# Second-layer steps of a two-layer graph attention kernel placed among the first layer's lists, with stored partial sums and a closing on ScalarE

## The chip, the cores and the metric

The kernel runs on one core of one Trainium2 chip. A core has five engines, each with an in-order queue of its own: TensorE (PE, matmuls; weight loads are listed as PEld), VectorE (DVE), ScalarE (ACT), GpSimd (POOL) and SyncE (SP), which here only issues transfers (DMA). The metric is device time in microseconds (us), the median of several runs.

## What is computed

There are 4096 nodes with 256 features and a sparse symmetric adjacency matrix (about one entry in 128 set, the diagonal always). Two graph attention layers follow each other, each with a residual and a layer norm:

```python
# layer 0: 8 heads of 128
Wh = einsum('nf,hfd->hnd', x, W_heads)
e  = leaky(s1[:, :, None] + s2[:, None, :], 0.2)     # s1, s2: Wh against a1, a2
att = softmax(where(adj > 0, e, NEG), axis=-1)
feat = elu(einsum('hnm,hmd->hnd', att, Wh))          # heads side by side
x = layernorm(x + feat @ W_out + b_out)
# layer 1: 4 heads of 64, the same adjacency
xt = einsum('ni,hio->hno', x, W)
e  = leaky(src[:, :, None] + dst[:, None, :], 0.2)
h  = einsum('hij,hjf->hif', softmax(where(adj > 0, e, -inf)), xt)
x = layernorm(x + heads side by side of h)
```

## The kernel before

In both layers the exponential of a leaky sum is taken as the larger of two products, so that a weight is two or three elementwise operations and no exponential for each pair. A row of ones beside the values gives the softmax's sums.

**First layer, sparse.** The 4096 targets are cut into 32 tiles of 128, each tile into 8 groups of 16 targets; a group is a *list* n = 0 to 255. For each list the nodes that are neighbours of any of its 16 targets are known as indices, and POOL gathers their table rows (256 features, factors, adjacency words: 305 floats) by indirect transfers: four of 128 rows for each list (`gather`, L777), and one more for four lists together (`Shared`, L791). DVE weighs them (`weigh`, L905 to L915), PE multiplies weights and rows into one PSUM bank (`gathered`, L918; L923), DVE inverts the sum and ACT divides (`invert`, `divide` L945, L947), PE transposes and ACT copies (`flip`, L950 to L957). The tile's own 128 rows come as `Near` (L835). When a tile's 8 lists are done, `close0` (L962) projects its heads (L981), applies elu, projects again (L1004), adds and normalises, and writes the tile's rows to DRAM (`x1_d`, L1028) and their transpose to `x1T` (L1032).

**Lists of neighbours.** For each of eight phases of 32 lists, `words_of` loads 16 blocks of adjacency (512 KB each, L508), turns them into 0 or 1 on ACT (two passes, L515 and L516) and packs the bits of 16 targets into words by matmuls (L528). `lists_of` picks the set nodes out of them on DVE (L594, L595) and publishes words and factors in the table.

**Order.** The first layer's order is written out by hand: one loop over n (L1097) emits, for each list, its pieces and those of neighbouring lists at fixed distances, a piece of counting, a piece of picking and one or two pieces of the queue `late`, which holds the closings and the second layer's scores and projections (`prepare1`, L744, L759, L768). Each engine gets its instructions in the order of this emission.

**Second layer, dense.** It begins when the loop has ended. For two pairs of heads g, four quarters of targets c (1024 each) and 32 source tiles j there is a *step*: load 512 KB of transposed adjacency on SP (L1181), turn it into an upper limit on ACT (L1182), weigh on DVE for both heads (L1310), and multiply on PE into three PSUM banks that accumulate over the 32 j: eight matmuls for values (L1200), four for sums (L1212), each of 32 columns, side by side in the array, each as two instructions. That is 256 steps. After each (g, c) the banks are copied, transposed back, divided and added to `y_sb` by DVE (`unit1`, L1222, L1250); with the second g each tile is normalised on DVE with a power on POOL (`layernorm`, L430 to L438) and stored. Here a scheduler orders the instructions.

The step's multiplications are these:

```python
for q in range(NQ):
    for b in range(2 * D1 // DQ):
        k, d = divmod(b * DQ, D1)
        nc.tensor.matmul(po[q][ts(b, DQ), :], wh[:, j, k, d : d + DQ],
                         es[k][:, ts(q, HB)], start=(j == 0), stop=(j == NT - 1), ...)
```

PSUM has eight banks: two each of `o0` (lists), `o1` (closings, scores) and `o2` (counting) in the pool `ps_o`, which the second layer uses for its sums, and two of `m` in `ps_m`.

Of the kernel before, what the change touches and what calls it, by code (L numbers as in the profile page):

```python
# [18 lines left out]
P = 128  # L19
# [243 lines left out]
def fast_path(  # L263
# [18 lines left out]
    CT = CH // P  # L282
# [21 lines left out]
    big = ctx.enter_context(tc.tile_pool(name="big", bufs=1))  # L304
    wpool = ctx.enter_context(tc.tile_pool(name="wh", bufs=1))
    apool = ctx.enter_context(tc.tile_pool(name="adj", bufs=4))
    small = ctx.enter_context(tc.tile_pool(name="small", bufs=4))
    ps_o = ctx.enter_context(tc.tile_pool(name="ps_o", bufs=2, space=PSUM))
    ps_m = ctx.enter_context(tc.tile_pool(name="ps_m", bufs=2, space=PSUM))
    first = ctx.enter_context(ExitStack())  # L310
    keep0 = first.enter_context(tc.tile_pool(name="keep0", bufs=1))
# [16 lines left out]
    xT_sb = big.tile([P, KC, N], F32, tag="xT", name="xT_sb")  # L328
    bad = const.tile([P, 6], F32, name="bad")
    nc.gpsimd.memset(bad, 0.0)  # L330
    rd_all = const.tile([P, NT * GT], F32, name="rd_all")

# [3 lines left out]
    class Scores:  # L336
# [38 lines left out]
        def chunk(self, k, src):  # L375
# [4 lines left out]
            def scores():  # L380
                ps = held["ps"] = ps_o.tile([P, CT, 2, H], F32, tag="o1", name=f"ps_{n}_{k}")
                for t in range(CT):
                    for c in range(KC):
                        nc.tensor.matmul(  # L384
                            ps[:, t],
                            src[:, c, ts(k * CT + t, P)],
                            self.v[:, c],
                            start=(c == 0),
                            stop=(c == KC - 1),
                        )  # L390
# [21 lines left out]
            def rows():  # L412
# [4 lines left out]
                nc.scalar.dma_start(self.r_d[k].rearrange("h t p -> (h t) p"), row)  # L417
# [11 lines left out]

    def layernorm(n, i, y):  # L430
        st = small.tile([P, nc.vector.BN_STATS_DIM], F32, tag="st", name=f"st_{n}_{i}")
        nc.vector.bn_stats(st, y)
        mv = small.tile([P, nc.vector.BN_AGGR_DIM], F32, tag="mv", name=f"mv_{n}_{i}")
        nc.vector.bn_aggr(mv, st)
        rstd = small.tile([P, 1], F32, tag="rstd", name=f"rstd_{n}_{i}")
        nc.vector.tensor_scalar(rstd, mv[:, 1:2], EPS, None, ALU.add)  # L436
        nc.gpsimd.tensor_tensor(rstd, rstd, neg_half, ALU.pow)  # L437
        nc.vector.tensor_scalar(y, y, mv[:, 0:1], rstd, ALU.subtract, ALU.mult)  # L438

# [58 lines left out]
    def words_of(s):  # L498

        pw = words[s] = []  # L500
        raw, bins = {}, {}
        NW = PT * NQ0

        def load(m):
            i, q = s * PT + m // NQ0, m % NQ0
            raw[m] = apool.tile([P, QN], I32, tag="aq", name=f"aq_{i}_{q}")
            queue = nc.scalar if s == 0 and m % 2 else nc.sync
            queue.dma_start(raw[m], adj[ts(i, P), ts(q, QN)])  # L508

        def convert(m):  # L510
            mb = two.tile([P, QN], BF16, tag="mb", name=f"mb_{s}_{m}", bufs=3)
            if s == 0:
                nc.vector.tensor_scalar(mb, raw.pop(m), 0.0, None, ALU.is_gt)
            else:
                nc.scalar.activation(mb, raw.pop(m), AF.Relu)  # L515
                nc.scalar.activation(mb, mb, AF.Sign)  # L516
            bins[m] = mb

        def count(m):

            t, q = divmod(m, NQ0)
            if m == 0:
                pw.extend(
                    ps_o.tile([P, 512], F32, tag="o2", name=f"pw_{s}_{k}") for k in range(QN // 512)
                )
            mb = bins.pop(m)
            for k in range(QN // 512):
                nc.tensor.matmul(  # L528
                    pw[k][ts(q, GP), :],
                    word[:, t, :],  # L530
                    mb[:, ts(k, 512)],
                    start=(t == 0),
                    stop=(t == PT - 1),
                    tile_position=(0, q * GP),
                    skip_group_check=True,
                )
# [861 lines left out]
```

## Time and profile before

| | us |
|---|---|
| median of three runs | 2705.93 (2693.68 to 2710.3) |
| span of the profiled execution | 2577.5 |
| first gather / last gather issued | 98 / 1779 |
| last list's matmuls begin | about 1803 |
| first / last matmul of the second layer | 1833 / 2555 |
| granted TensorE clock, mean | 0.924 |

The span runs from the first to the last instruction of one profiled execution; the timed runs are some 128 us longer. Busy time over the span: PE 2186.5 us (85%), DVE 1854.4 (72%), POOL 1201.6 (47%), ACT 1029.5 (40%). A matmul's listed duration contains its latency and overlaps the next one's, so PE's pace is read from counts in a stretch rather than from durations. In the rows below "idle before" is the time that the engine stood idle ahead of such an instruction, with what ended it.

### The profile page before, as it was taken

Reading aid. Unit: us, or ns where it says so; the run is one execution under the profiler, and the core shown is the slowest. Engines: PE = TensorE matmul, PEld = TensorE weight load, DVE = VectorE, ACT = ScalarE, POOL = GpSimd, SP = SyncE. Lnnn points to the kernel's source line nnn. Section 1 sums busy time; section 2 is a strip of 40 time slices with the busy share of each in tenths; the row PEclk is TensorE's granted clock in tenths of the full one; section 3 lists DMA queues with packets and bytes.
Section 4 is the critical chain, followed back from the end, with each engine's and each line's share of the span. In section 5 each row is a group of like instructions: output and inputs, shape, how many; then the busy total and the mean of one; then the engine's idle time right before and its main releaser. Section 6 shows DMA issues by size and latency. Waiting matters only on the chain.

```text
span 2577.5 us, 37206 instructions
## 1 busy us (share of the span) xinstructions
PE 2186.5 (85%) x12585; PEld 1281.6 (50%) x12585; DVE 1854.4 (72%) x3802; ACT 1029.5 (40%) x2577; POOL 1201.6 (47%) x1156
## 2 busy tenths in 40 slices
PE   6368888888878888888788887878999999999997
PEld 4235565555555555556555565655543432324433
DVE  4547668667656667755776766555699799999997
ACT  0075535435533543553453233332444544334332
POOL 1356677677566677657767767774000000010110
PEclk9978889999888898888998989998999999999998
DMA  9597556557455646655765644442766566666653
GB/s 279 148 299 181 164 156 188 161 158 192 136 151 135 203 132 154 193 143 139 199 182 147 134 115 137 120 129 75 241 223 195 165 203 211 210 200 220 190 179 98
DMA packets 212958, 443.64 MB, mean 172 GB/s; under 512 B 60819, under 2 KB 125462, under 8 KB 212758
## 3 DMA queue, kind: packets, MB, share of 16 engines
q1 hardware_dynamic: 152982, 261.55, 34.4%
q0 software_dynamic: 52224, 169.97, 23.2%
q10 hardware_dynamic: 7552, 9.65, 1.1%
q8 instruction: 102, 1.67, 0.3%
q14 instruction: 98, 0.80, 0.1%
HBM read 426.04 MB, written 23.40 MB: 174 GB/s over the span
## 4 chain that ended last, share of the span: by engine, by line
PE 61%; DMA 14%; DVE 10%; ACT 6%; POOL 4%; issue 4%; ACTq 0%; DVEq 0%; POOLq 0%; SPq 0%
PE po L923 24%; PE po L1200 17%; DMA G<-table,ids 12%; PE po L1212 8%; POOL G L783 3%; PE ph L981 3%; PE py L1004 3%; ACT ag L947 2%; PE pw L528 2%; PE ps L384 2%; DVE e L908 1%; DVE e L914 1%; DVE e L915 1%; PE pw L759 1%; ACT el L991 1%
## 5 line engine op out<-in xcount | busy, mean ns | idle before, releaser
L783 POOL DMA_INDIRECT G<-table,ids x1024 | 1083.4, 1058 | 586.3 <-issue 354.3
L1310 DVE SCALAR_TENSOR_TENSOR e<-rb,pj,mb 128x1024 f32<-128x1024 f32 x512 | 631.2, 1279 | 44.3 <-PE po L1212 24.4
L923 PE MATMUL po<-G,e 128*128 128x257 f32 x2048 | 620.5, 455 | 13.1 <-DVE e L915 12.9
L1200 PE MATMUL po<-e,wh 128*32 128x512 f32 x4096 | 623.5, 594 | 6.5 <-DVE e L1310 6.0
L923 PEld LDWEIGHTS po<-G,e 128*128 128x128 f32 x2048 | 433.3, 222 | 179.3 <-issue 38.3
L1212 PE MATMUL po<-e,cj 128*32 128x512 f32 x2048 | 464.2, 592 | 0.0
L1182 ACT ACTIVATE mb<-aq 128x1024 bf16<-128x1024 int32 x256 | 270.7, 1058 | 412.9 <-DVE e L1310 353.3
L923 PE MATMUL po<-own,eo 128*128 128x257 f32 x512 | 184.5, 444 | 285.9 <-ACT ag L947 271.0
L437 POOL TENSOR_TENSOR rstd<-rstd,neg_half 128x1 f32<-128x1 f32 x32 | 28.4, 891 | 722.9 <-DVE rstd L436 533.7
L1200 PEld LDWEIGHTS po<-e,wh 128*32 128x32 f32 x4096 | 199.9, 110 | 281.7 <-issue 196.3
L923 PEld LDWEIGHTS po<-own,eo 128*128 128x128 f32 x512 | 82.3, 202 | 324.9 <-ACT ag L947 310.4
L915 DVE TENSOR_TENSOR e<-e,mbs 128x512 f32<-128x512 f32 x256 | 177.4, 693 | 65.9 <-ACT mbs L902 43.4
L923 PE MATMUL po<-Gs,e_s 32*128 32x257 f32 x512 | 196.2, 465 | 8.0 <-DVE e_s L833 8.0
L1212 PEld LDWEIGHTS po<-e,cj 128*32 128x32 f32 x2048 | 126.6, 110 | 139.3 <-issue 117.0
L914 DVE TENSOR_TENSOR e<-e,G 128x512 f32<-128x512 f32 x256 | 177.5, 693 | 8.7
L957 ACT COPY aT<-pa 128x256 f32<-128x256 f32 x256 | 94.2, 369 | 218.7 <-PE pa L954 218.4
L908 DVE TENSOR_TENSOR e<-rb,G 128x512 f32<-128x512 f32 x256 | 177.8, 694 | 4.5 <-issue 0.7
L947 ACT ACTIVATE ag<-po,rd_all 128x256 f32<-128x256 f32 x256 | 120.7, 471 | 125.0 <-DVE rd_all L943 124.7
L886 ACT CAST w<-G 128x4 int32<-128x4 f32 x256 | 48.8, 191 | 259.8 <-DMA G<-table,ids 248.0
L981 PEld LDWEIGHTS ph<-aT,w_sb 128*128 128x128 f32 x1024 | 134.2, 201 | 20.2 <-issue 14.8
L981 PE MATMUL ph<-aT,w_sb 128*128 128x128 f32 x1024 | 140.9, 287 | 0.5 <-ACT aT L957 0.5
L853 DVE TENSOR_TENSOR nbo<-wo,bit 128x128 int32<-128x128 int32 x32 | 9.6, 299 | 174.5 <-ACT wo L851 174.5
(160 smaller groups left out, 2360.0 us busy)
## 6 DMA issues: line engine op xcount, KB each, us to landing
aq<-in_adjT SPq DMA_DIRECT2D x256, 512.0 KB, 4.7
aq<-in_adj SPq DMA_DIRECT2D x120, 512.0 KB, 6.3
rb<-r_d SPq DMA_DIRECT2D x48, 512.0 KB, 9.0
G<-table,ids POOLq DMA_INDIRECT x1024, 3.4
table<-in_x SPq DMA_DIRECT2D x8, 1024.0 KB, 11.6
table<-tail SPq DMA_DIRECT2D x56, 98.0 KB, 5.1
own<-table SPq DMA_DIRECT2D x32, 152.5 KB, 9.2
aq<-in_adj ACTq DMA_DIRECT2D x8, 512.0 KB, 7.9
```

The costliest lines, as they stand in the source:

```text
L783: nc.gpsimd.indirect_dma_start(out=G[:, b, :], out_offset=None, in_=table[s % 2][:, :], in_offset=bass.IndirectOffsetOnAxis(ap=lists[s][:, ...
L908: nc.vector.tensor_tensor(e, rb[:, :, ts(n % GT, T)].unsqueeze(1).to_broadcast(sh), G[:, :, CC:QQ].unsqueeze(3).to_broadcast(sh), ALU.mult,)
L914: nc.vector.tensor_tensor(e, e, G[:, :, QQ:WD].unsqueeze(3).to_broadcast(sh), ALU.max)
L915: nc.vector.tensor_tensor(e, e, mb.unsqueeze(2).to_broadcast(sh), ALU.min)
L923: nc.tensor.matmul(po, w.rearrange("p h t -> p (h t)"), v[:, 0 : F + 1], start=first, **kw)
L947: nc.scalar.activation(ag, po[:, 0:F], AF.Copy, scale=rd_all[:, n : n + 1])
L957: nc.scalar.copy(aT[:, :, :, ts(n % GT, T)], pt)
L981: nc.tensor.matmul(phs[k][:, hh, :], w_sb[:, c, ts(h, D0)], aT[:, c, h, :], start=(c == 0), stop=(c == KC - 1),)
L1182: nc.scalar.activation(mb, aq, AF.Relu, scale=OPEN)
L1200: nc.tensor.matmul(po[q][ts(b, DQ), :], wh[:, j, k, d : d + DQ], es[k][:, ts(q, HB)], start=(j == 0), stop=(j == NT - 1), tile_position=(0 ...
L1212: nc.tensor.matmul(po[NQ][r0 : r0 + DQ, :], sc1.cj[:, j, 2 * g + k : 2 * g + k + 1].to_broadcast([P, DQ]), es[k][:, ts(q, HB)], start=(j = ...
L1310: nc.vector.scalar_tensor_tensor(e, rb[k], sc1.pj[:, j, h : h + 1], mb, ALU.max, ALU.min)
```

## The change

The second layer no longer waits for the whole first layer. When eight tiles (a quarter of the nodes) are closed, their rows can be sources and targets, so `Dense.release(q)` queues the steps that only need finished quarters: all sources so far for targets of quarter q, and sources of quarter q for the earlier quarters. That gives 16, 48, 80 and 112 steps. One is taken in each turn of the first layer's loop, its four pieces (load, mask, weigh, multiply) in successive turns; the multiplication stands ahead of the list's own. What is left when the loop ends runs in a loop of its own, also in the written order.

```diff
+        def release(self, q):
+            for c in range(q + 1):
+                for g in range(G1):
+                    j0, j1 = (0, (q + 1) * CT) if c == q else (q * CT, (q + 1) * CT)
+                    part = {"g": g, "c": c, "last": q == NCH - 1, "q": q}
+                    for j in range(j0, j1):
+                        self.steps.append((part, j, j == j0, j == j1 - 1))
+        def load(self):
+            part, j, first, last = s = self.steps.pop(0)
+            if first:
...
+                    t = self.near.tile([P, CH], F32, tag="rb", ...)
+                    nc.sync.dma_start(t, r.to_broadcast([P, CH]))
+            aq = self.adj.tile([P, CH], I32, tag="aq1", ...)
+            nc.sync.dma_start(aq, adjT[ts(j, P), ts(c, CH)])
+            wh = self.near.tile([P, 2 * D1], F32, tag="wh", ..., bufs=5)
+            nc.sync.dma_start(wh, wh_d[g, j])
...
+        def ready(self):
+            if not self.steps or len(self.loaded) > 1:
+                return False
+            return not self.steps[0][2] or not (self.loaded or self.masked)
```

In the loop over n (the mask is L1111 in the new numbering, the weighing L1121, the multiplications L1140 and L1152):

```diff
+            step = bool(dense.more())
+            if step and dense.weighed:
+                dense.multiply()
             if n < NG:
                 G = rows.pop(n)
                 e = weigh(n, G, near[i].rb, masks.pop(n))
                 sums[n] = (gathered(n, G, e, near[i], shared[n // SL]), aT)
+            if step:
+                if dense.masked:
+                    dense.weigh()
+                if dense.loaded:
+                    dense.mask()
+                while dense.ready():
+                    dense.load()
...
-            late.some(2 if n % GT in (1, 5) else 1)
+            late.some(2 if n % 2 else 1)
```

A run of steps with one (g, c) and one released quarter is a *part*; there are 20. Its three banks are copied by ACT; unless the part belongs to the last quarter they are stored to DRAM. At the end the parts of a (g, c) are loaded again and joined by matmuls against the identity (`together`):

```diff
+            for q in (NQ, 0, 1):
+                t = self.sum.tile([P, HB], F32, tag="h1", ...)
+                nc.scalar.copy(t, po[q])
+                hs.append(t)
+            if part["last"]:
+                self.ends.append((g, c, hs))
+            else:
+                o = dram.tile([NQ + 1, P, HB], F32, ...)
+                for k, t in enumerate(hs):
+                    nc.sync.dma_start(o[k], t)
...
+        def together(pt, q, cols, right):
+            for m, part in enumerate(parts):
+                nc.tensor.matmul(pt, part[q][:, cols], right,
+                                 start=(m == 0), stop=(m == len(parts) - 1))
```

The closing of the second layer scales on ACT and adds four tiles at once on DVE; mean, squares and normalisation are ACT passes of 256 elements with an accumulated output, two quarters of a chunk at a time:

```diff
-                    nc.vector.scalar_tensor_tensor(
-                        y, pt[:, k, a, :], rd[:, k, a, q : q + 1], y, ALU.mult, ALU.add
+                    nc.scalar.activation(
+                        z[:, k, a], pt[:, k, a], AF.Copy, scale=rd[:, k, a, q : q + 1]
                     )
+            nc.vector.tensor_tensor(y, y, z.rearrange("p k a d -> p k (a d)"), ALU.add)
...
+                nc.scalar.activation(o, y, AF.Copy, accum_out=st[:, 0, k : k + 1])
...
+                    o, y, AF.Square, bias=st[:, 0, k : k + 1], accum_out=st[:, 1, k : k + 1]
...
+                    y, y, AF.Identity, scale=st[:, 1, k : k + 1], bias=st[:, 2, k : k + 1]
```

Around it:

- PSUM: the second layer has three banks of its own (`ps_d`, one buffer each); `o1` has one buffer where it had two, and counting moves from `o2` to `m`.
- Counting: a block of adjacency is now one target tile by 256 columns of each quarter (runs of 1 KB where they were 4 KB, 512 KB a block as before), ACT makes it -1 or 1 in one pass (`Sign` with a bias), and the matmuls of four blocks, 16 a tile by 256 columns, follow each other over the four column groups; ACT's copy undoes the -1.
- The second layer's scores and projections are made for four tiles at a time as soon as these are closed, both pairs of heads at once (`project1`), and the projected rows go to DRAM (`wh_d`), from where each step loads 64 KB. The transposed rows of all nodes are no longer kept.
- The small stores of closed rows and of the scores' rows are issued by SP where ACT issued them.
- The adjacency's pool has three buffers where it had four; the dense steps have two of their own in the loop and four behind it. The first layer's opening loads the transposed input in four pieces through two buffers.

## The prediction

> **What bounds the kernel now.** I read the busy shares by slice first, then a table of engine time by stage, then the waits, then the chain of waits inside one stretch. The page's slices show two stages; the second begins where POOL goes quiet.
>
> ```profile
> span 2577.5 us, 37206 instructions
> PE   6368888888878888888788887878999999999997
> DVE  4547668667656667755776766555699799999997
> POOL 1356677677566677657767767774000000010110
> PEclk9978889999888898888998989998999999999998
> ...
> 1024.00:1280.00 256.00, 212.99 (x907) 143.95 (x905) 176.83 (x462) 116.40 (x338) 171.61 (x166) 0.90 0.61 166
> 1536.00:1792.00 256.00, 206.56 (x912) 149.61 (x911) 145.02 (x350) 78.98 (x308) 182.03 (x170) 0.90 0.44 120
> 2100.00:2300.00 200.00, 199.77 (x1816) 60.63 (x1808) 191.48 (x208) 81.57 (x83) 3.65 (x3) 1.00 0.66 212
> ```
>
> Columns of the last three: stretch, length, busy us (and count) of PE, weight loads, DVE, ACT, POOL, then granted clock, DMA share, GB/s. In the first layer nothing is full: PE is busy 83%, at a granted clock of 0.90, DVE 57 to 69%. In the second PE is full at clock 1.00 and DVE at 96%; POOL idles. Why PE has gaps in the first layer:
>
> ```profile
> POOL G L783 <- issue: 354.3, 797, 6.5
> PE po L923 <- ACT ag L947: 271.0, 150, 7.2
> ACT w L886 <- DMA G<-table,ids: 248.0, 79, 8.4
> ...
> 927.23 2.99 PE po L923 x12
> 943.88 6.10 PE po L923 x12
> ```
>
> PE's next list waits for the division of the list two before it (L947), which stands on ACT behind a word copy (L886) that waits for gathered rows. The last two lines, from the chain of waits, are the same twelve matmuls: 2.99 us without a gap ahead of them, 6.10 us after one. So the first layer is bound by its loop of gathers: POOL gives 4.25 gathers a list, each 1.06 us and 0.30 to the next, 5.8 us of the 6.2 to 6.7 us that a list takes (461 matmuls of L923 from 1024 to 1280 us, twelve a list, give 6.66; 496 from 1536 to 1792 give 6.19: I use 6.65 and 6.2).
>
> ```profile
> L1310 DVE SCALAR_TENSOR_TENSOR e<-rb,pj,mb 128x1024 f32<-128x1024 f32 x512 | 631.2, 1279 | 44.3 <-PE po L1212 24.4
> L1182 ACT ACTIVATE mb<-aq 128x1024 bf16<-128x1024 int32 x256 | 270.7, 1058 | 412.9 <-DVE e L1310 353.3
> 1840.00:1900.00 60.00, 60.00 (x564) 27.65 (x560) 0.00 (x0) 0.00 (x0) 1.00 0.80 273
> ```
>
> These price one second-layer step. The last line counts its matmuls alone: 564, at 24 a step, in 60 us, or 2.55 us of PE a step. DVE needs two times 1.28, 2.56 us; ACT 1.06 us.
>
> **The change part by part.** *Steps moved.* In the changed program's TensorE order 16 steps stand before the gathered matmuls of lists 82 to 98, 48 before those of 146 to 196, 41 before those of 210 to 254: 105 among the lists, 151 behind the last.
>
> What a list with a step takes: PE's own work for a list, at the pace without gaps, is 2.99 (gathered), 0.22 (transposes), 0.55 (heads: 1.09 for eight, four a list), 0.48 and 0.08 (projection: 1.92 for eight, two a list, and bias), and about 0.4 for the rest, 4.75 us. With a step it is 7.3 us. DVE's is 0.69 x 6.65 = 4.6 us while the next lists are picked, 0.57 x 6.2 = 3.5 at the end; with a step 7.2 and 6.1. POOL's stays 5.8. So PE becomes the bound, close to DVE in the first 64 steps. Two in-order engines at their limit lose something to each other: the old second stage took 722 us (1833 to 2555) for 256 steps, 2.82 against 2.55, a tenth. I take 7.3 x 1.1 = 8.0 us for 64 lists and 7.3 x 1.05 = 7.7 for 41. Added: 64 x 1.35 + 41 x 1.5 = 148 us.
>
> *The clock rule.* The row: 2.99 or 6.10 us for one list's matmuls, and 0.90 against 1.00 by stage. The Trainium skill, TensorE: Matmul & The Clock Gate, Part 1, says that the clock halves after an idle window of about 3.4 us and returns after a busy one. By the average row PE's work is about 83% of 6.65, 5.5 us, and a list with a step is at least 8.05 us before any loss; by the rule the step, which stands just where PE waits for L947, fills the gap, keeps the clock, and 4.75 + 2.55 counts. I follow the rule, with the clock of 1.00 in the full stage for it; the other costs 0.75 x 105 = 79 us more and is in the range.
>
> *A rule against the change.* The step's DVE instruction reads two operands in SBUF. The Trainium skill, SBUF — State Buffer, Who interferes with whom, says that such an instruction and a GpSimd one that reads SBUF exclude each other, the later one blocked in full. By it each list's gathers could lose up to 2.56 us: 5.8 + 2.56 = 8.4 us, POOL the bound again, some 0.5 x 105 = 50 us more. The row: in 30 us windows of this trace a gather took 0.95 to 0.98 us where DVE was busy 13 us, 1.02 where it was busy 27.9. I go by the row and leave the 50 us in the range.
>
> *What the moved steps bring to the queues.* SP gets, for each step, the 512 KB of adjacency as before and now 64 KB of projected rows, for each of 20 parts two broadcast rows of 512 KB (40, were 16), the stores of unfinished sums (36 of 256 KB), and the two small stores that ACT's queue had. Extra bytes: 17 + 9 + 9 back + 4 + 13 = 52 MB; at the 284 GB/s which the gather queue reached (170 MB in 23.2% of the engines' span) 180 us of transfer at a DMA share of 0.44 to 0.61: hidden, if SP issues in time. A step's load goes out two lists before ACT reads it, 16 us, against 4.7 us to landing. The exception is a part's first load: the rows' buffers are two, so SP waits for DVE's last weighing of the part before, with the next adjacency load, Near's loads and the stores behind it; then ACT's mask is due one list later, 8 us, behind 1.5 MB (5.3 us) and a landing. ACT may stand there, and with it the admission of the next list and L947. Bounds 0 and 3 us at 11 starts; I take 1: 11 us.
>
> *The last stage.* From list 255's matmuls (1803) to the end the old program took 775 us. Now: 151 x 2.55 = 385; joining sums, 20 parts of about 3.3 us (16 instructions at 0.135 and eight weight loads of 0.14), 66, where 8 parts took 26 and 17 us of projections (L759) have left the stage; first-layer rest 10. That is 461 us, where the old stage had 256 x 2.55 = 653 + 26 + 17 = 696 in its 722 us: a share of 0.964, so 478. Loading y (4 MB, at 280 GB/s 15 us, ahead of the next adjacency loads on SP) and the verdict's chain, which PE waits for, cost 12 with three steps in flight as cover, 25 without. The end takes 22 as before, 2555 to 2577. Together 512: 263 us gone.
>
> *Closing on ScalarE* takes 26 us (L1250) and 37 us (normalising) off DVE, gives it 11, and gives ACT 128 scalings at 0.33 and 96 passes at 0.47, 87 us, on top of 151 x 1.06 + 14 of about 490 us: covered by ACT's idle time. PE bounds the stage, so I count nothing; without cover it would be the last chunk's 12 us or so.
>
> *Counting.* One ACT pass of 1.06 us less for each of 112 blocks, and matmuls of four column groups side by side in place of one group after another: at most 60 us of PE (0.54 a block) and 118 of ACT, at least nothing, since gathers bound those lists. I take 20. Runs of 1 KB in the adjacency may lengthen the opening: 0 to 12 us (the gathers' 1.2 KB runs went at full rate), I take 5. The single buffer of L977 makes PE wait for ACT and DVE where two late pieces fall in one list, 0 to 60 us over all; the neighbouring step covers it, and it is part of the tenth above.
>
> *Sum*: 148 + 11 + 5 - 20 - 263 = -119 us on a span of 2577.5: 2459. The timed median, 2705.93, lies 128 us above the span; I carry these 128, which no row explains, over unchanged: about 2590 us.
>
> **Rivals.** *Full overlap*: no loss of a tenth, 7.3 us a list, 64 x 0.7 + 41 x 0.4 = 61 us less: 2525. For it: POOL needs 5.8 and DVE 6.1 to 7.2. Against: no stage here reached it. *Plain addition*: gaps and clock stay and a list takes 2.55 us more; 105 x 2.55 = 268 us in place of 148 eats the gain: 2710. For it: the gaps come from gathers that land late (up to 13.3 us), which more traffic does not help. Against: a list later is also more time for a gather. *ACT's queue stops behind the mask*: L1111 stands ahead of the admission of each next list, its load on an SP that now waits for ACT, DVE and PE in one order. If it stands there, ag and the next list stand, PE's clock falls, and a list takes 10.5 us: 64 x 3.85 + 41 x 4.3 = 423 in place of 148, so 2590 + 275 = 2865, slower. It decides from 2.5 us more a list, about 9 us, where the 263 us are spent. For it: SP already waits 683 us for DVE at Near's rows. Against: two lists of lead. That the steps don't get among the lists is excluded by the instruction order.
>
> **How the numbers follow.** My forecast 0.50, full overlap 0.15, plain addition 0.15, ACT stopped 0.20. What cannot be told from no change is 1%, 2679 to 2733. Faster: 0.48 + 0.15 + 0.04 = 0.67; same 0.12; slower 0.21. The forecast alone spans 2520 to 2670; the range, with most of the first and second rival and the lower part of the third, 2500 to 2770.
>
> **What would show it.** Right: about 8 us between lists where steps stand, 6.5 elsewhere, granted clock near 1.00 there, PE's wait for L947 gone, 151 steps in some 490 us. Wrong: lists of 9 us and more, ACT waiting for adjacency, gathers landing at 8 us with PE waiting, or a last stage over 550 us.

## The result, and the profile after

| | before | after |
|---|---|---|
| median of four runs each, us | 2699.8 (2686.08 to 2710.3) | 2878.85 (2858.49 to 2886.41) |
| ratio | | 1.067, interval 1.0602 to 1.0738 |
| span of the profiled execution, us | 2693.3 (profiled again, e1 below) | 2884.6 |

The kernel became 6.7% slower, where 2590 us had been forecast. Each trace is of one execution, and those of e2 and e3 below are of slow ones, 40 and 29 us above the medians of their kernels' fast runs. The first lines of the new page (span, busy time and share of each engine, slices of TensorE and of its granted clock):

```profile
span 2884.6 us, 38591 instructions
PE 2285.9 (79%) x13101; PEld 1331.4 (46%) x13101; DVE 1813.5 (63%) x3610; ACT 1011.0 (35%) x2817; POOL 1215.3 (42%) x1134
...
PE   3367778787879777777878898778988978878997
...
PEclk9968887877889789889889899989898989888998
```

No engine is full over the span. The old last stage, whose twelve or so slices stood at nine tenths and full clock, is gone; most of what replaced it stands at seven to nine tenths. The split of the time comes from the first and the last start of a list's first matmul. Here are these rows of the groups by line, before (profiled again) and after:

```profile
L923 PE MATMUL po<-own,eo x512: 379/383/797, 110.3 to 1916.4; 128*128 128x257 f32 x171
```

```profile
L923 PE MATMUL po<-own,eo x512: 380/484/797, 128.9 to 2261.9; 128*128 128x257 f32 x171
```

The lists begin 19 us later, take 2133 us in place of 1806, and what follows the last one takes 2884.6 - 2261.9 = 623 us in place of 777: +19 + 327 - 154 = 191 us, the difference of the two spans. The prediction had +5, +139 (steps 148 + 11, counting -20) and -263. All three terms were wrong on the same side. By the starts in the trace, the lists at the places that the prediction gave to the steps (82 to 98, 146 to 196, 210 to 254) took 9.3 us each on the mean, the others 7.7; it had 7.7 to 8.0 and 6.2 to 6.65.

Where engines stood, from the waits of the whole span (releaser; us, times, longest):

```profile
PE po L923 <- ACT ag L947: 191.6, 65, 15.3
DVE e L1121 <- PE po L1152: 146.1, 61, 7.2
ACT h L1170 <- DMA part<-h: 79.0, 10, 14.1
ACT mb L1111 <- DMA aq<-in_adjT: 68.1, 37, 13.4
```

The first wait was to go; it is smaller than before (264.0 us, longest 12.0, in e1) and its longest piece has grown. The third is new and was in no term of the sum: of the three banks of a finished part the third copy needs a buffer of the pool of two (`sum1`) that the first store must have emptied. Nine of these ten waits, 71.6 us, fall before the last list's matmuls; the timeline shows the tenth, in the turns just behind the last list, which use the same pool (start, length, engine, what; idle time ahead of it in brackets):

```profile
2324.82 0.58 ACT L1170 COPY h<-po 128x512 f32<-128x512 f32 x1 [1.45 <-PE po L1140]
2325.68 0.58 ACT L1170 COPY h<-po 128x512 f32<-128x512 f32 x1 [0.27 <-PE po L1152]
...
2327.07 7.49 SPq L1177 DMA_DIRECT2D part<-h  x3
2333.62 0.58 ACT L1170 COPY h<-po 128x512 f32<-128x512 f32 x1 [7.36 <-DMA part<-h]
...
2335.20 2.48 DVE L1121 SCALAR_TENSOR_TENSOR e<-rb,pj,mb 128x1024 f32<-128x1024 f32 x2 [11.53 <-ACT mb L1111]
...
2336.54 2.27 PE L1140 MATMUL po<-e,cj 128*32 128x512 f32 x6 [8.16 <-DVE e L1121]
```

ScalarE stands 7.4 us, the next mask is behind that copy, VectorE stands 11.5 us for the mask and TensorE 8.2 us for VectorE. In the list loop ScalarE's work for the next list is behind it too.

The same stretch of lists without steps (e1) and with them (the changed kernel), columns as in the prediction's windows:

```profile
1300.00:1700.00 400.00, 322.20 (x1346) 223.56 (x1344) 264.66 (x684) 143.17 (x474) 265.69 (x251) 0.87 0.52 139
```

```profile
1300.00:1700.00 400.00, 333.90 (x1964) 184.38 (x1956) 274.19 (x537) 147.74 (x396) 198.15 (x179) 0.89 0.63 178
```

And the last stage of the changed kernel, mostly its short parts and then its long ones:

```profile
2330.00:2700.00 370.00, 307.75 (x2352) 145.75 (x2352) 207.54 (x215) 147.97 (x330) 11.45 (x6) 0.87 0.62 200
2700.00:2860.00 160.00, 156.07 (x1384) 47.75 (x1384) 137.44 (x119) 66.78 (x83) 0.17 (x1) 0.99 0.67 210
```

With steps among the lists the clock is 0.89, against 0.87 without, and TensorE is idle 66 us of the 400 where it was idle 78: the steps fill few of the gaps. Counted by L1152, 16 to a step, the first stretch of the last stage holds 79 steps, 4.7 us each, the second 56.6, 2.8 each. The starts in the trace show where the time goes: of the six parts of eight steps, five begin 13 to 20 us behind the step ahead of them, their next three steps take 4 to 7 us each, and the others 2.6 to 2.9.

### The profile page after: what moved, and what is told of

It is laid out like the page before. It is cut to its first block, busy times and chain, and to the rows that moved or that the text cites. A ratio compares the mean times of both kernels' runs of the same rounds, so it can differ in the third digit from the quotient of the medians.

```text
span 2884.6 us, 38591 instructions
## 1 busy us (share of the span) xinstructions
PE 2285.9 (79%) x13101; PEld 1331.4 (46%) x13101; DVE 1813.5 (63%) x3610; ACT 1011.0 (35%) x2817; POOL 1215.3 (42%) x1134
## 5 line engine op out<-in xcount | busy, mean ns | idle before, releaser
L783 POOL DMA_INDIRECT G<-table,ids x1024 | 1110.3, 1084 | 988.7 <-issue 563.2
L1121 DVE SCALAR_TENSOR_TENSOR e<-rb,pj,mb 128x1024 f32<-128x1024 f32 x512 | 634.1, 1279 | 276.5 <-PE po L1152 146.1
L923 PE MATMUL po<-G,e 128*128 128x257 f32 x2048 | 611.6, 449 | 7.6 <-DVE e L915 5.4
L1152 PE MATMUL po<-e,wh 128*32 128x512 f32 x4096 | 584.4, 607 | 0.0
L923 PE MATMUL po<-own,eo 128*128 128x257 f32 x512 | 198.8, 474 | 282.7 <-ACT ag L947 191.6
L1140 PE MATMUL po<-e,cj 128*32 128x512 f32 x2048 | 386.9, 634 | 33.1 <-DVE e L1121 30.5
L1111 ACT ACTIVATE mb<-aq 128x1024 bf16<-128x1024 int32 x256 | 271.2, 1063 | 165.7 <-DVE e L1121 78.0
L1152 PEld LDWEIGHTS po<-e,wh 128*32 128x32 f32 x4096 | 168.5, 113 | 310.9 <-issue 290.2
L1380 POOL TENSOR_TENSOR st<-st,neg_half 128x4 f32<-128x4 f32 x8 | 13.6, 1704 | 546.9 <-DVE st L1379 545.9
L902 ACT ACTIVATE mbs<-nb 128x64 f32<-128x64 int32 x256 | 66.6, 260 | 324.0 <-DVE nb L891 273.8
L1004 PE MATMUL py<-wo_sb,hT 128*128 128x256 f32 x512 | 152.4, 451 | 0.0
L1140 PEld LDWEIGHTS po<-e,cj 128*32 128x32 f32 x2048 | 73.7, 111 | 147.1 <-DVE e L1121 84.8
```

Source lines behind the costliest of these rows:

```text
L783: nc.gpsimd.indirect_dma_start(out=G[:, b, :], out_offset=None, in_=table[s % 2][:, :], in_offset=bass.IndirectOffsetOnAxis(ap=lists[s][:, ...
L923: nc.tensor.matmul(po, w.rearrange("p h t -> p (h t)"), v[:, 0 : F + 1], start=first, **kw)
L1004: nc.tensor.matmul(pys[0], hT[:, h, :], wo_sb[:, h, :], start=False, stop=(h == H0 - 1))
L1111: nc.scalar.activation(mb, aq, AF.Relu, scale=OPEN)
L1121: nc.vector.scalar_tensor_tensor(e, part["rb"][k], sc1.pj[:, j, h : h + 1], mb, ALU.max, ALU.min)
L1140: nc.tensor.matmul(po[NQ][r0 : r0 + DQ, :], sc1.cj[:, j, 2 * g + k : 2 * g + k + 1].to_broadcast([P, DQ]), es[k][:, ts(q, HB)], start=star ...
```

## The experiments

Each ratio is to the kernel before, run in the same set. The sets differ: in those of e1 to e15 the kernel before takes 2684 to 2700 us, in those of e16 to e18 2577 and 2579; only ratios are compared across them. "Lists" is the time from the first to the last list's first matmul, divided by 255; "last stage" is from there to the end of the span.

| | ratio (interval) | first list at | us a list | last stage |
|---|---|---|---|---|
| before (e1) | | 110.3 | 7.08 | 777 |
| after | 1.067 (1.0602 to 1.0738) | 128.9 | 8.36 | 623 |
| e2 no steps in the loop | 1.0997 (1.0933 to 1.1061) | 128.4 | 7.50 | 952 |
| e3 third copy later | 1.0394 (1.029 to 1.0499) | 130.5 | 8.10 | 619 |
| e4 no start-up at borders | 1.0568 (1.0514 to 1.0623) | 128.7 | 8.25 | 602 |
| e5 as e2, elu apart | 1.117 (1.1081 to 1.1258) | 127.3 | 7.52 | 957 |
| e6 as e2, count copy later | 1.1117 (1.1035 to 1.1198) | 127.6 | 7.60 | 944 |
| e7 as e2, stores on ACT | 1.1073 (1.0982 to 1.1165) | 124.5 | 7.47 | 951 |
| e8 e4 and longer leads | 1.0483 (1.0406 to 1.056) | 128.0 | 8.37 | 581 |
| e9 as e2, old counting | 1.1049 (1.0981 to 1.1117) | 131.8 | 7.37 | 950 |
| e10 e3 and e8 | 1.0348 (1.0278 to 1.0418) | 129.0 | 8.02 | 582 |
| e11 e10, words early | 1.0235 (1.0162 to 1.0309) | 129.9 | 7.93 | 582 |
| e12 as e2, no projection | 1.1037 (1.0975 to 1.1098) | 127.0 | 7.45 | 932 |
| e13 as e2, score rows later | 1.1082 (1.1016 to 1.1148) | 127.3 | 7.32 | 952 |
| e14 e11, pairs on even turns | 1.0164 (1.0105 to 1.0222) | 128.6 | 7.91 | 585 |
| e15 before, words early | 0.9982 (0.9944 to 1.0019) | 108.7 | 7.05 | 778 |
| e16 as e2, four undone | 1.1006 (1.0949 to 1.1063) | 123.4 | 6.88 | 955 |
| e17 e14, joining in three turns | 1.0083 (1.0058 to 1.0108) | 128.5 | 7.33 | 589 |
| e18 e17, transfers in time | 0.9879 (0.984 to 0.9919) | 127.0 | 7.40 | 533 |

Lists of the changed loop that no edit touched (after, e4, e8) differ by 0.12 us, 30 us over the loop; smaller differences in that column are not read.

**What the kernel before takes, and what the steps cost (e1, e2).** e1 is the kernel before, unchanged.

> The kernel before, unchanged, profiled once more: its timed runs lie 128 us above the span of the profile that the prediction was read from. If those 128 us are list time, this execution has a span of about 2700 and its lists take about 7.0 us in place of 6.65 and 6.2, the second layer staying near 722 us. If they lie outside the span, the span is again about 2580 and lists take 6.65.

One run, 2695.13 us, its span 2693.3. So almost nothing lies outside the span: the execution that the prediction was read from was a quick one, with a clock of 0.924 in place of 0.899. Lists take 7.08 us in place of 6.63, 115 us over 255; the second layer's 723 us at clock 1.00 are the same. The prediction put these 128 us on top of its sum; nearly all of them are list time.

```diff
-            step = bool(dense.more())
+            step = False
```

> The changed kernel with no step among the lists: all 256 run in the loop behind the last list. Theory that the steps themselves slow the lists: lists fall back to about 7.0 us, the last one is done near 1900 us, and 256 steps at the rate of the changed kernel's last stage (151 in 600 us, 4.0 us each) take about 1000, together about 2900. Rival, that something else in the changed first layer (counting in narrow blocks, one closing buffer, stores on SP) slows it: lists stay at 7.4 us and above through the whole loop, last one near 2000 us, together 3000. In either case the list time of the stretch 200 to 800 us, which holds no steps in both, should stay at 7.4 us and a granted clock of 0.81.

```profile
L923 PE MATMUL po<-own,eo x512: 380/383/797, 128.4 to 2040.5; 128*128 128x257 f32 x171
```

1912 us of lists without a single step, against 1806 before: the changed first layer is itself 106 us longer, and 18 us later; up to 40 of the 106 may be this one execution's own. With e2 as the base, the 105 steps cost 2133 - 1912 = 221 us, 2.1 each (up to 2.5 if those 40 us are taken off the base), where 1.35 and 1.5 had been predicted. And 256 steps behind the lists take 952 us where the old stage took 777: the new last stage is worse by 175 us before anything is overlapped. The median of 2957.61 lies between the two expectations: lists stay near 7.5 us through the whole loop (7.7 between 200 and 800 us, 7.3 at the end), as the rival had it.

**The third copy (e3).** The third copy and its store move to the next turn, where `finish` emits them (`out1(k)` copies bank k and stores it); nothing else changes.

```diff
+            out1(0)
+            out1(1)
+            if self.sum is sum1:
+                self.third.append(lambda: out1(2))
...
+            dense.finish()
             step = bool(dense.more())
```

> The third bank of a finished part is copied one turn of the loop later, when the first of the two sum buffers has been stored. Theory that ScalarE stands at the third copy until a store has landed, with all engines behind it, about 8 us for each of 12 stored parts: 80 to 100 us less, about 2790, and the waits of the copy for its store are nearly gone. Rival, that the lists have other work of their own that is late at the same places (gathers, TensorE): less than 25 us gained, about 2865.

```profile
ACT h L1177 <- DMA part<-h: 19.4, 3, 9.9
```

The wait falls from 79.0 to 19.4 us, the ratio from 1.067 to 1.0394: about 2.8%, some 70 us. That is a little less than expected, and in the traces nearly all of it is among the lists: 2066 us in place of 2133. Against e2's 1912 a step then costs (2066 - 1912) / 105 = 1.47 us, or 1.6 if what both executions have above their medians is list time: the size that the prediction had.

**Borders and leads in the last stage (e4, e8).**

```diff
         def ready(self):
...
+            if self.near is not near1:
+                return True
             return not self.steps[0][2] or not (self.loaded or self.masked)
```

> In the stage behind the lists, the first load of a part no longer waits until the part before it has been masked; nothing else is changed. Theory that the six parts of eight steps each lose a start-up (load of 1.5 MB, mask, weigh, some 9 us) at every border, with which 2330 to 2700 us ran at 4.3 us a step and 2700 to 2860 at 2.6: about 60 us less, 2820. Rival 1, that the joining pieces between two steps hold DVE up: less than 20 us gained. Rival 2, that loads issued only two steps ahead land late: less than 20 us gained, and ScalarE still waits for adjacency.

The last stage falls from 623 to 602 us, a third of what was expected; ScalarE still waits 90.2 us for adjacency.

```diff
-            pools = (("adj2", 4), ("near2", 4), ("weight2", 6), ("sum2", 6))
+            pools = (("adj2", 6), ("near2", 4), ("weight2", 8), ("sum2", 6))
+            self.lead, self.nwh = 3, 8
...
-            if not self.steps or len(self.loaded) > 1:
+            if not self.steps or len(self.loaded) > self.lead:
...
-            if dense.weighed:
+            if len(dense.weighed) > (1 if dense.masked else 0):
```

> As e4 (no start-up at part borders behind the lists), and there adjacency is loaded up to four steps ahead in place of two, and VectorE weighs one step further ahead of TensorE. Theory that late loads and the joining pieces hold the last stage up beside the borders: its 151 steps take about 480 us in place of 560, total 60 to 80 us below e4, near 2765. Rival, that with the borders gone the stage is bound by TensorE and the joining matmuls: less than 20 us below e4.

The wait for adjacency goes to 30.5 us, the stage only to 581. Neither the theory of 480 us nor its rival, a stage bound by TensorE, was right: something else stood there.

**Why lists without steps are longer (e5, e6, e7, e9, e12, e13, e16).** All are e2 with one part of the changed first layer undone (e16 with four).

```diff
-            lambda: (project(0), elu(1)),
-            lambda: project(1),
+            lambda: elu(1),
+            lambda: None,
+            lambda: (project(0), project(1)),
```

> As e2 (no step among the lists), and the second elu stands two pieces ahead of the second projection, so that TensorE does not stand at the single closing buffer until ScalarE and VectorE are done. Theory that this buffer is a main part of the 0.4 us by which the changed lists are longer than the old ones (e2 7.48, before 7.07; TensorE stood 54 us at L1002 in 1700 us): TensorE's wait at L1002 goes, lists about 7.3 us, total 50 us below e2, near 2910. Rival, that the lists are bound elsewhere (gathers, ScalarE's order): the wait goes and the lists stay at 7.45, total within 15 us of e2.

TensorE's wait at L1002 (54.0 us between 200 and 1900 us in e2) is gone, the lists take 7.52 us and the ratio is no lower: that wait is slack. ScalarE's wait for the inverted sum grew from 148.6 to 179.7 us.

e6, where the counting piece also moves to the end of the turn:

```diff
-                nc.scalar.activation(o, pw, AF.Identity, scale=0.5, bias=less[:, 1:2])
+                copies.add(lambda: nc.scalar.activation(o, pw, AF.Identity, ...))
...
                 flip(n - 3, ag, done)
+            copies.all()
```

> As e2, with the counting piece put last in a turn and the copy of its bank emitted in the next turn, behind the transposed list's copy. In e2 ScalarE stood some 92 us of 1700 at that copy (L540) until TensorE had worked its queue off, with the next list's words and division behind it. Theory that this stand is a main part of the 0.4 us: it goes, lists 7.25 to 7.3 us, total 40 to 60 us below e2. Rival, that ScalarE's stand is slack: the next wait takes its place, lists 7.45, total within 15 us of e2.

ScalarE no longer stands there (52.0 us for the matmul alone in e2); lists 7.60. Slack too.

e7:

```diff
-                nc.sync.dma_start(self.r_d[a // CQ, :, ds(a % CQ, CT), :], row)
+                nc.scalar.dma_start(self.r_d[a // CQ, :, ds(a % CQ, CT), :], row)
...
-            nc.sync.dma_start(x1_d[ii], y)
+            nc.scalar.dma_start(x1_d[ii], y)
```

> As e2, with the stores of closed rows and of score rows issued from ScalarE's queue as before the change, not from SP. Theory that SP, standing at these stores for VectorE, lets later loads go out late: first list at 110 us in place of 128, lists 7.3 us or less, total 40 to 60 us below e2. Rival, that SP has slack behind them except in the opening: first list 5 to 18 us earlier, lists unchanged at 7.45, total 5 to 20 us below e2.

The rival: the first list comes 4 us earlier, the lists are as before.

e9, `words_of` and its copies as in the kernel before, with two banks of the pool `ps_d`, idle here:

```diff
-            queue.dma_start(raw[m], adj[ts(s * PT + t, P), :].rearrange(...)[:, :, ts(k, W)])
+            queue.dma_start(raw[m], adj[ts(i, P), ts(q, QN)])
...
-                nc.scalar.activation(mb, raw.pop(m), AF.Sign, bias=less[:, 0:1])
+                nc.scalar.activation(mb, raw.pop(m), AF.Relu)
+                nc.scalar.activation(mb, mb, AF.Sign)
...
-            pw = ps_m.tile([P, W], F32, tag="m", ...)
+                    ps_d.tile([P, 512], F32, tag=f"d{k}", ...) for k in range(QN // 512)
```

> As e2 (no step among the lists), with the counting of the kernel before: contiguous 512 KB loads, two passes on ScalarE, two matmuls of 512 columns in each piece, two banks held for a phase. In e2 the lists 8 to 23 of a phase, which hold the counting, take 7.9 us against 7.2 in the kernel before, the lists 24 to 31 of a phase 6.6 in both. Theory that the new counting makes the lists longer: lists back at 7.1 us, total 80 to 100 us below e2, about 2880. Rival, that the second layer's extra pieces (scores for four tiles at a time, projection of all heads, two late pieces in every second turn) do it: lists 7.4 us, total within 25 us of e2 or above it, since the second pass on ScalarE is back.

7.37 us a list, no gain in time: the new counting is not the loss, and the 20 us that the prediction gave to it are not seen either (1.1049 against 1.0997, the intervals overlap). The first list comes at 131.8 us, no earlier than in e2: the 1 KB runs of the new loads, to which the prediction gave the opening's 5 us, are not what delays it.

e12:

```diff
-                late.add(*(lambda m=m: project1(m) for m in range(s * PT, s * PT + PT)))
...
-            nc.sync.dma_start(wh, wh_d[g, j])
+            nc.sync.dma_start(wh, x1_d[j, :, ts(g, 2 * D1)])
```

> As e2 (no step among the lists); the projection of the closed rows for the second layer is left out (the steps multiply with rows of x1 of the same size), so eight pieces in eight tiles are gone, each with two weight loads and two matmuls of 256 columns and four scalings on ScalarE. Theory that the added pieces lengthen the lists: lists 7.2 us, total 70 us or more below e2. Rival, that they fit in idle time: lists 7.4 or more, total within 25 us of e2.

Lists 7.45: the projections fit in idle time.

e13, the copy and its store emitted in the next turn:

```diff
-                nc.vector.tensor_copy(row, pr)
+                copies.add(out)
...
+            copies.all()
             if n >= 3:
                 ag, done = means.pop(n - 3)
```

> As e2, and VectorE copies the transposed score rows out of their bank one turn later (in e2 it stood 6.6 us at each of them, 0.4 us a list in the lists 8 to 23 of a phase, for TensorE to work its queue off). Theory that this stand, with ScalarE's wait for the inverted sum behind it (0.7 us a list, 0.2 before), is a main part of the 0.4 us: lists 7.25, total 30 to 60 us below e2. Rival, slack: the stand goes, total within 20 us of e2.

VectorE still stood 35.9 us there (39.6 in e2): the edit did not remove what it was to remove, and its 7.32 us a list show nothing about that stand.

e16: e7, e9 and e13 together, the second projection in a bank of its own, and no steps while the last late pieces run:

```diff
-                pys.append(ps_o.tile([P, F], F32, tag="o1", ...))
+                pys.append(ps_d.tile([P, F], F32, tag="d2", ...))
```

> As e2 (no step among the lists) with counting as before, a bank of its own for the second projection (TensorE no longer waits for the elu at L1002), score rows copied a turn later and the small stores on ScalarE's queue. Theory that the loss of 0.4 us a list is the sum of these: lists 7.1 us, first list near 112 us, total 90 to 110 us below e2. Rival, that it lies in the two late pieces in every second turn and the clock that falls with TensorE's gaps: lists 7.3, total 40 to 60 us below e2.

Lists 6.88 us. In this set the kernel before takes 2577 us, the time of the execution with 6.63 us a list, so 0.25 us remain of 0.42. That the four are worth something together where none was alone is likely and not shown: e2 was not run in this set, its 0.42 contain up to 0.16 of its execution, and the ratio, 1.1006, is that of e2. One reason for the ratio is known: this kernel runs no steps while it empties its queue of late pieces, and the first step follows the last list by 58 us, in e2 by 11.

The other 0.25 us were not traced to one part, and one part stood in all of these runs: the two late pieces in every second turn, which e16's rival named. By the starts in the traces (the first tile left out), the intervals behind places 1, 2 and 3 of a tile are 0.7, 1.1 and 1.4 us longer in e16 than in the first profile of the kernel before, and 0.4, 1.7 and 2.3 longer in e2 than in e1; place 3 has two late pieces where it had one. That points there; no run undid it.

**All repairs together (e10, e11, e14, e15).**

> The two repairs together, with the steps among the lists: third copy a turn later (e3, ratio 1.039) and the last stage without borders and with longer leads (e8, ratio 1.048; the changed kernel 1.067 to 1.07). If both waits are separate they add: 2879 - 60 - 50, ratio about 1.02 to the kernel before. If one hides the other: 1.035 or more.

1.035: e3 took 0.028 off the ratio and e8 0.019, together they took 0.032, a difference that lies within the intervals. In the trace both savings are there: 8.02 us a list as in e3, a last stage of 582 us as in e8.

```diff
+                if n % GT == 4:
+                    near[i + 1].words() 
-                if n % GT == 5:
+                elif n % GT == 5:
                     near[i + 1].admit()
```

> As e10, and ScalarE copies the words of a tile's own rows one turn before VectorE needs them (VectorE stood some 120 us at L853 in e2, and the list at place 5 of a tile took 10.7 us where others took 7). Theory that this stand lengthens every eighth list: the list at place 5 falls to about 8, 32 times 2.5 us, ratio about 0.99. Rival, that the near rows' weighing itself is what lengthens that list: within 20 us of e10.

VectorE's wait at L853 is gone (84.7 us in e10). The median is 32 us lower; the intervals overlap, and the list at place 5 of a tile still takes 10.7 us: it is not the words that lengthen it. Nor is it the change: in e1, the kernel before, place 5 takes 10.5 us too.

```diff
-            late.some(2 if n % 2 else 1)
+            late.some(1 if n % 2 else 2)
```

> As e11, with the two late pieces in even turns in place of odd ones, so that the last heads, their elu and the projection that reads it no longer stand in one turn (place 5 of a tile, which takes 10.7 us in e11). Theory that this chain through TensorE, ScalarE, VectorE and TensorE in one turn lengthens place 5: place 5 falls to 8 or 9 us and the total by 30 to 60 us, ratio 1.00 to 1.01. Rival, that the same chain only moves to another place: ratio unchanged at 1.02.

The mean intervals between lists by place in a tile, from the starts in the trace: place 5 falls to 8.2 us, but places 4 and 6 rise to 9.7 and 10.3. The chain moved; the median is 15 us lower, the intervals overlap.

> The kernel before with the early copy of the near rows' words alone, which gave 12 to 50 us in e11. Theory that it is worth as much there, since VectorE stands at the same place (95 us at L853 in 1700 us of e1): ratio 0.98 to 0.99. Rival, that the stand is slack where TensorE has no steps: ratio 0.995 to 1.005.

No change where no steps stand: the words' stand is slack there.

**What held the last stage (e17, e18).** e17 takes the joining apart: `settle`, called in each turn behind mask and weighing, emits the scalings of the turn before and the additions of the turn before that.

```diff
-            for k in range(nt):
-                for a in range(2):
-                    nc.scalar.activation(
+            after1.append((scale1, add1))
...
+            settle()
             late.some(1)
```

> As e14, with each joining piece of the last stage taken apart: TensorE's part in one turn, ScalarE's scaling in the next behind the mask, VectorE's addition in the one after behind the weighing; and the score rows copied a turn later (e13). Theory that the last stage stands in these pieces (ScalarE waited 103 us for the joined sums with the masks behind it, VectorE 61 us for ScalarE): the stage falls by 60 to 100 us, ratio 0.98 to 0.995. Rival, that TensorE's joining and the late loads bound it: the waits move, ratio 1.00 to 1.015.

The stage is 589 us, no shorter: the rival. The ratio is 0.8 hundredths lower; the intervals touch, and the sets of e14 and e17 differ, so this gain is not shown. The chain of waits of e17, in order of time (start, length, what), then names what was left:

```profile
...
2168.48 5.95 DMA aq<-in_adjT
2174.45 9.87 DMA part_sb<-part
2184.36 5.71 PE pd L1376 x26
2190.07 1.87 PE po L1154 x8
```

TensorE's wait for stored parts in the whole span of e17:

```profile
PE pd L1376 <- DMA part_sb<-part: 27.0, 12, 4.2
```

The chain goes through the load of a stored part, 9.87 us, of which the joining matmuls were emitted one turn behind the issue, and through loads of adjacency that follow the 4 MB of y on one queue.

```diff
+        if len(parts) > 1:
+            late.add(*[lambda: None] * 3)
         late.add(dens)
...
-        for c in range(NCH):
-            nc.sync.dma_start(y_sb[:, ts(c, CT), :], ...)
...
         while dense.more():
+            if turns % 8 == 0 and turns // 8 < NCH:
+                c = turns // 8
+                nc.sync.dma_start(y_sb[:, ts(c, CT), :], ...)
```

> As e17, and the joining of a unit begins three turns after its stored parts' loads were issued, and y is loaded in four pieces eight turns apart in place of 4 MB at once. Theory that the last stage stands for these transfers: the stage from the last list to the end falls from 589 us to about 530, ratio 0.98 to 0.99. Rival, that TensorE's own work (152 steps at 2.55, joining 68, the end 25: 480 us) with VectorE behind it bounds the stage: less than 20 us, ratio 1.00 to 1.01.

The stage falls to 533 us, as expected, and the kernel is now 1.2% faster than the one before: 2546.98 against 2579.33 us, ratio 0.9879 (0.984 to 0.9919). That is in a set where the kernel before is quick; in the other kind it was not run. The two edits, delayed joining and y in pieces, were not run apart; TensorE's wait for stored parts, which went, was 27 of the 56 us. That wait, and the short parts' stretch of the last stage with its continuation, in e18:

```profile
PE pd L1376 <- DMA part_sb<-part: 0.5, 1, 0.5
```

```profile
2050.00:2350.00 300.00, 287.33 (x2418) 120.14 (x2417) 219.98 (x223) 140.91 (x274) 9.41 (x5) 0.98 0.76 260
2350.00:2520.00 170.00, 169.53 (x1542) 57.23 (x1544) 146.53 (x133) 82.11 (x148) 3.82 (x2) 1.00 0.63 203
```

TensorE is busy 96% at a clock of 0.98 where it was busy 83% at 0.87: only now is it what bounds this stage.

## Why the prediction was wrong

The sum had -119 us for the span and +191 came, 310 more. By e1, e2 and the changed kernel: 126 lie in lists without steps (+106 for -20), 14 in the opening, 62 in what the steps cost (221 for 159) and 109 in the last stage (-154 for -263). Up to 40 of the 126 may be e2's own execution and would then belong to the steps.

*The bound.* That TensorE has gaps in the first layer and none in the second was right. That a step would fill the gaps was right in small part: a step took 2.1 us among the lists against 2.8 in the old stage (723 / 256), but TensorE's idle time in the window above only fell from 78 to 66 us of 400.

*Steps among the lists, 1.35 and 1.5 us.* The size was right and one wait was missing. "What the moved steps bring to the queues" priced SP's loads and issues; it did not ask how many buffers the three copies of a finished part have. With the third copy moved a step costs 1.5 to 1.6 us (e3 against e2). The missing term is some 70 us. The eleven waits at a part's first load, priced at 11 us, are not there: among the lists of the changed kernel no mask waits for adjacency, and all 68.1 us of that wait in the rows above lie behind the last list.

*Counting -20, opening +5, closing buffer at nothing.* Together they were to take 15 us off; e2 shows +106 in the lists and +18 in the opening. This is the step that failed most: the first layer's new pieces were costed by their busy time and by TensorE's waits, one by one. Each of five edits that undid one part moved the list time by less than 0.2 us and none lowered the ratio (e5, e6, e7, e9, e12); with four undone 0.25 us of 0.42 were left, in another set (e16). The cause stays open; the two late pieces in every second turn, which the prediction knew and put with the closing buffer, are the part not undone. Of the opening, 4 us went back with the stores (e7), none with the loads of 4 KB runs (e9); in the changed kernel's first 135 us POOL's first gathers are released by the store of a score row on SP, which stands behind loads that wait for the two buffers of `xT`, but no run moved those loads.

*Last stage, 512 us.* It took 623. Joining was sized rightly: in e17's chain a unit of four parts costs 5.71 + 3.77 + 3.77 us (the two joins of values are rows of the same chain), near four times the 3.3 that the sum had. "Three steps in flight as cover" failed: borders and leads were worth 42 us (e8 against the changed kernel), and the loads of stored parts and of y 56 (e17 to e18). Bringing the sums back was costed as matmuls and as bytes on the queue, never as a transfer that TensorE waits for at a fixed place. With these repaired the stage is 533, within 21 us of the sum.

*Closing on ScalarE at nothing.* With the scalings taken out of VectorE's and TensorE's way (e17) the stage was no shorter, which speaks for it. The closing was not undone by itself.

*The clock rule.* The prediction followed the Trainium skill (TensorE: Matmul & The Clock Gate, Part 1) against the row, and expected 1.00. The row was nearer: 0.89 in the window above, 0.87 in e1 between 1300 and 1700 us without steps. The steps did not fill the gaps (66 us idle for 78), so the premise failed before the rule did. Nor do long gaps alone explain the clock: in the changed kernel's window the clock in the trace is either 1.00 or 0.50, at 0.50 in twelve stretches, 85 us together, and TensorE stands more than 3.4 us only four times. Where TensorE is truly fed (e18's last stage, 0.98 to 1.00) the rule's clock appears.

*The port rule, put aside.* Rightly as to size: gathers take 1058 ns on the mean in the first profile, 1058 in e2 without steps beside them and 1084 with them. The mean hides an effect, though. Sorted by the trace, the 188 gathers that overlap a step's weighing took 1210 ns and the other 836 took 1056: something slows them there (the port or the steps' transfers, the runs do not tell), 29 us of POOL in all, far from an exclusion for two times 1.28 us in each of 105 lists and inside the 50 us that the range held.

*The 128 us* were carried over in the right size for the runs, with a wrong place: most of them are list time (115 of the 116 us between the two profiles).

*The rivals.* "ACT's queue stops", 2865 us, came nearest to 2878.85. Its mechanism, a ScalarE that stands with everything behind it, is there, among the lists at the sums' third copy and not at the mask, and it explains some 70 of the 310 us. The rest is the longer lists and the last stage, which no rival named; that its number came so near is luck. (Full overlap's sum is 2590 - 61 = 2529 us, not 2525; nothing hangs on it.)

## What to carry to other kernels

When work is moved among other work, count the buffers of every small pool on its way out as well as in, and ask of each copy, store and load which instruction stands for it and what is queued behind that instruction; busy times and bytes do not show it. A stage that a scheduler used to order and that is now written out by hand needs its leads sized against the measured landing times (here about 10 us against a turn of 2.6), at every transfer and not at the main one alone. Before a part is costed at nothing, run it alone: a kernel with everything but the overlap (e2) shows at once how much of the change has nothing to do with the overlap.

## What was not expected of the hardware

The same kernel takes 2577 us in some sets of runs and 2684 to 2700 in others. Nearly all of it lies where TensorE has gaps: list time 6.63 against 7.08 us at clocks of 0.89 and 0.86 in the windows 100 to 1800 us, while the full stage takes 723 us in both. It is not spread evenly: the median interval between lists is 6.6 us in both profiles, and of the 115 us some 77 stand behind place 5 of a tile, 10.4 us for 8.1 on the mean of 32 tiles. Why one place should differ between sets stays open. A single profile can therefore sit 4% away from the times beside it.

Waits that look large in a table can be slack: 54 us of TensorE, 93 of ScalarE (L540, all releasers) and 85 of VectorE were removed one at a time (e5, e6, e11); the first two gave nothing, the third 1% within overlapping intervals.
